# Four graph layers on one core: layer 2's squares ahead of the roots from the seventh group of a block, and four degree sums moved from layer 0 to layer 1

## The chip, the cores and the metric

The kernel runs on one core of a Trainium2 chip. The metric is the device time of one launch in microseconds (us). The kernel before took 1160.33 us (median of 3 runs, 1156.4 to 1161.47).

## The reference

Four graph layers over N = 4096 nodes with 64 features share one dense adjacency matrix `adj` (4096 x 4096, float32). Each layer takes `h = relu(layernorm(x))` and adds its result to `x`. Cut to what matters:

```
# layer 0
x = x + relu((adj @ h) @ W.T + b)
# layer 1: h, q, k are Lorentz-linear maps (each of 64 features)
att = adj * sigmoid((2 + 2 * (qm @ k.T)) / att_scale + att_bias)
support = att @ h;  x = x + support / sqrt(max(|-inner(support)|, 1e-8))
# layer 2: Poincare ball; log_ij is the log map of node j at node i
deg = max(adj.sum(axis=1), 1e-8);  w = adj / deg
agg = einsum('ij,ijc->ic', w, log_ij)     # norm of (-x_i) (+) x_j, arctanh of it, direction
x = x + expmap(0, agg @ weight + bias)
# layer 3: rank of each nonzero within its row; the last 100 weigh 0.5 ** (k - pos)
x = x + (w(rank) @ (h @ weight) + bias)
```

Layer 2 needs for every pair of nodes a scalar: with a squared distance quantity in PSUM it is worked out as square, clamp, log, square root, inverse square root (exponentials of plus and minus half the log), sum with the signed distance, log again, product. Layer 2 also needs `deg`, the row sums of `adj`. These are gathered while layers 0 and 1 read the matrix anyway.

## The kernel before, in words

The 4096 target nodes are cut into NB = 8 blocks of W = 512. The source nodes are cut into NG = 16 groups of 256 (G = 2 times 128). One adjacency tile is 128 x 2 x 512 floats, 512 KB, and belongs to one block `ib` and one group `g`.

**Tiles and loads.** `feed` (line 804) issues one DMA per tile on SyncE's queue (SP). In layers 0 and 1 the tiles live in two pools: `adjp` (6 buffers, line 156) and `adj01` (4, line 848). In each pool buffers are used in turn, and `feed` takes the pool whose oldest tile comes free first (`oldest`, line 798). A tile counts its users in `left` (`group`, line 856): its products or sums, and one more if its degree sum is made in that layer. Nineteen small DMAs for constants go out on ScalarE's queue (`constants`, line 928) while the first block runs.

**Layer 0.** `l0_sums` multiplies each tile with `h` on TensorE (PE) into an accumulator. `degree_sums(0, ...)` (line 890) adds the tile to a running tile `dg` on VectorE (DVE): a copy for a block's first tile, an addition for each further one. At a block's end `after0` (line 566) turns the sum over partitions into `deg` with one-column matmuls, and `before1` prepares layer 1's rows of this block.

**Layer 1.** `l1_atts` (PE), `l1_sigmoids` (ScalarE, ACT), `l1_weights` (DVE, `sig` times adj), `l1_sums` (PE). Some degree sums are done here: groups 3, 7, 11 and 15 (`LEFT`) of blocks 1 to 6. Where a block has such sums, `after1` (line 591) adds two `dg` halves, makes eight more one-column matmuls (each of four is issued as a pair) and adds to `deg`. The last 12 groups of layer 0 alternate with the first 12 groups of layer 1 (`EARLY`), whose blocks 0 and 1 run side by side.

**Layer 2.** The pairs are symmetric, so a block `ib` works on groups of target blocks J = ib to 7 only: 16, 14, 12, ... 2 groups, 72 in all. The first two of each block lie on the diagonal; the second of these is half as wide. Each other group is used twice: as it is, and transposed. The stages of a group:

- PE: `l2_dists` into one of two PSUM buffers `mm`; `l2_signs` into the same buffer after the square
- ACT: `l2_squares` (`v<-mm`); POOL: `l2_clamps` (`v<-v`); ACT: `l2_first_logs` (`v<-v,minus`), `l2_roots` (`t<-v`), `l2_inverses` (`v<-v`)
- DVE: `l2_coshs` (`t<-mm,t`), which frees the `mm` buffer; ACT: `l2_logs` (`t<-t`); DVE: `l2_pairs` (`t<-t,v`), `l2_weights` (`w<-t,adj`)
- PE: `l2_sums`; `l2_turns` (transposes); DVE: `l2_weights2` (`w<-tr,adj`, twice); PE: `l2_sums2`; DVE or ACT: `l2_gathers` (`others`) once per two groups

**What sets the order.** Each engine runs its instructions in program order. `in_turn` (line 733) writes this order: every stage is a thread, a cost model (`Pace`, line 60) says when each could start, and the earliest goes next. `in_steps` (line 1266) ties several threads of one engine into a fixed order per step: step k of ACT is first log k, root k, square k + 1, inverse k, log k; of DVE pair k - 1, weight k - 1, cosh k, turned weights k - 1; of PE distances k + 1, signs k, turned sums k - 2, transposes k - 1, sums k - 1. The work after a block (`after2`, `before3`) is placed between these by the planner.

Nearly all instructions are recorded by the profile under line 132, a helper that all engines share, so they are told apart by tile names.

Of the kernel before, what the change touches and what calls it, by code (L numbers as in the profile page):

```python
# [23 lines left out]
NB = N // W  # L24
CB = W // P
G = 2
NG = NC // G
LEFT = (3, 7, 11, 15)
WAIT = 0.6
EARLY = 12  # L30
BEHIND = NG - CB // G
LATE = BEHIND - CB // G
# [107 lines left out]
def kernel(ctx: ExitStack, tc: tile.TileContext, a: dict, out: bass.AP):  # L140
# [589 lines left out]
    def latest(*times):  # L730
        return None if None in times else max(times)
# [36 lines left out]
    def keep_warm(wait):  # L768


        if wait < WAIT or not spare or l1[0].get("dist") and "tables" not in opened or "third" in opened:
            return
# [69 lines left out]
    def pair_buffer(name, k):  # L842
        return pairp.tile([P, G, W], F32, tag=f"pair{k % 2}", name=name)
# [10 lines left out]


    def group(layer, ib, g):
        degree = (g in LEFT and 0 < ib < NB - 1) == (layer == 1)
        return {"layer": layer, "ib": ib, "g": g, "degree": degree, "left": 1 + degree, "at": 0.0}

    l0 = [group(0, ib, g) for ib in range(NB) for g in range(NG)]
    l1 = [group(1, ib, g) for ib in range(2) for g in range(BEHIND)]
    l1 += [group(1, ib, g) for ib in range(2) for g in range(BEHIND, NG)]
    l1 += [group(1, ib, g) for ib in range(2, NB) for g in range(NG)]
    order = l0[: len(l0) - EARLY] + [d for pair in zip(l0[len(l0) - EARLY :], l1) for d in pair]
    order += l1[EARLY:]
    done = {}
# [107 lines left out]
    def l1_sums():  # L976
        for pair in pairs:
# [24 lines left out]
    work = [  # L1002
        {"ib": i, "J": j, "half": s, "g": j * (CB // G) + s, "first": i == j and s == 0,
         "last": j == NB - 1 and s == CB // G - 1, "two": i < j, "cut": i == j and s == 1,
         "left": 1 + (i == j and s == 1), "at": 0.0}
        for i in range(NB) for j in range(i, NB) for s in range(CB // G)
    ]
# [5 lines left out]
    def part(d, t):  # L1013
        return t[:, :, OWN:] if d["cut"] else t
# [4 lines left out]
    def ago(items, k, n, what):  # L1019

        return items[k - n].get(what) if k >= n else 0.0
# [44 lines left out]
    def l2_squares():  # L1066
        for k, d in enumerate(work):
            yield "ACT", lambda: latest(
                d.get("dist"), l1[2 * k - SIG].get("summed") if 2 * k < SIG else 0.0,
                ago(work, k, SIG // 2, "paired"),  # L1070
            )
            d["v"] = pair_buffer("v", 0)
            ACT.activation(part(d, d["v"]), part(d, d["ps"]), AF.Square)
            d["square"] = pace.latest
# [19 lines left out]
    def l2_first_logs():  # L1094
        for d in work:
            yield "ACT", lambda: latest(d.get("clamped"), opened.get("tables"))
            v = part(d, d["v"])
            ACT.activation(v, v, AF.Ln, bias=minus)
            d["first_log"] = pace.latest

    def l2_roots():
        for k, d in enumerate(work):
            yield "ACT", lambda: latest(
                d.get("first_log"),
                l1[2 * k + 1 - SIG].get("summed") if 2 * k < SIG else 0.0,
                ago(work, k, SIG // 2, "weighed"), ago(work, k, SIG // 2, "turned"),
            )
            d["t"] = pair_buffer("t", 1)
            ACT.activation(part(d, d["t"]), part(d, d["v"]), AF.Exp, scale=0.5)
            d["root"] = pace.latest  # L1110

    def l2_inverses():
        for d in work:
            yield "ACT", lambda: d.get("root")
            v = part(d, d["v"])
            ACT.activation(v, v, AF.Exp, scale=-0.5)
            d["inverse"] = pace.latest
# [8 lines left out]
    def l2_logs():  # L1126
        for d in work:
            yield "ACT", lambda: d.get("read")
            ACT.activation(part(d, d["t"]), part(d, d["t"]), AF.Ln, scale=2.0 / SC)
            d["log"] = pace.latest  # L1130
# [135 lines left out]
    def in_steps(*stages):  # L1266


        parts = [next(stage[0], None) for stage in stages]
        for step in range(-1, len(work) + 3):  # L1270
            for n, (gen, behind, many) in enumerate(stages):
                k = step - behind
                for _ in range(many(work[k]) if 0 <= k < len(work) else 0):
                    yield parts[n]
                    parts[n] = next(gen, None)

    def once(d):
        return 1

# [75 lines left out]
    def l3_counts():  # L1355


        totals = []
        for h in range(2 * NB):
            half = l3[h * HG : (h + 1) * HG]  # L1360
            yield "PE", lambda: latest(*(d.get("masked") for d in half)) if spare else None
            ps = bank()
            for k in range(KH):
                for r in range(4):
                    c = 4 * k + r
                    PE.matmul(
                        ps[r * Q : (r + 1) * Q, :], pick[:, k, :],
                        half[::-1][c // G]["m"][:, c % G, :],
                        start=(k == 0), stop=(k == KH - 1), skip_group_check=True,
                    )  # L1370
            yield "DVE", lambda: ready(ps)
            totals = (totals if h % 2 else []) + [(1 - h % 2, l3_copy(f"total{h % 2}", ps))]
            yield "PE", lambda: ready(totals[-1][1]) if spare else None
            ps = bank()
            for n, (i, t) in enumerate(totals):
                PE.matmul(
                    ps, spread[:, i, :, :].rearrange("p q c -> p (q c)"), t,
                    start=(n == 0), stop=(n == len(totals) - 1),
                )
            yield "DVE", lambda: latest(ready(ps), ago(l3, h * HG, HG + 1, "ranked"))  # L1380
            chunks = l3_copy("chunks", ps)
            for d in half:
                d["chunks"] = chunks
# [72 lines left out]
    def l3_sum():  # L1456
# [22 lines left out]
        if d["last"]:  # L1479
# [6 lines left out]
        l0_sums(), l1_sums(), l1_weights(), l1_sigmoids(), l1_atts(),  # L1486
        in_steps(
            (l2_dists(), -1, once), (l2_signs(), 0, once), (l2_sums2(), 2, if_two(1)),
            (l2_turns(), 1, lambda d: 2 if d["two"] else 1), (l2_sums(), 1, once),
        ),  # L1490
        in_steps(
            (l2_first_logs(), 0, once), (l2_roots(), 0, once), (l2_squares(), -1, once), (l2_inverses(), 0, once), (l2_logs(), 0, once),
        ),
        l3_counts(),
        in_steps(
            (l2_pairs(), 1, once), (l2_weights(), 1, once),
# [50 lines left out]
```

## Time and profile before

| | us |
|---|---|
| median of 3 runs | 1160.33 |
| the profiled execution | 1154.0 |
| its span, first to last instruction | 1152.3 |
| PE matmul busy | 1076.0 (93%) |
| VectorE busy | 914.3 (79%) |
| ScalarE busy | 785.0 (68%) |
| POOL busy | 285.7 (25%) |
| DMA moved | 271.77 MB, mean 236 GB/s |
| granted TensorE clock | 0.992 |

The engines' shares are means over four layers with different limits: layer 0 to about 200 us, layer 1 to about 465, layer 2 to about 940, layer 3 to the end. So they are read by stretch. `PEld` is the weight load of TensorE, which overlaps matmuls. In lists of instructions each line gives start, duration, engine, operation, output and inputs, and in brackets the idle time before it and what ended it. "issue" in a chain is time in which the engine at that point waited for nothing that the profile shows: it was working through earlier instructions.

### The profile page before, as it was taken

The numbers are of one execution on the slowest core, as the hardware profiler recorded it, in microseconds if no ns is written. First come the engines' busy times: TensorE is split into PE (matmuls) and PEld (weight loads), VectorE is DVE, ScalarE is ACT, GpSimd is POOL, SyncE is SP. The second block draws the span as 40 slices with busy tenths as digits, with TensorE's granted clock in tenths as the row PEclk, the third lists the DMA queues.
The fourth block names the chain that finished last, engine by engine and source line by source line (L and its number), as shares of the span: only waits on it lengthen the run. The fifth ranks groups of instructions, "written<-read, shape, count | busy, mean of one in ns | idle before, by whom it ended". The sixth has DMA issues, their size and how long they took to land.

```text
span 1152.3 us, 15824 instructions
## 1 busy us (share of the span) xinstructions
PE 1076.0 (93%) x5496; PEld 451.4 (39%) x5496; DVE 914.3 (79%) x1473; ACT 785.0 (68%) x1286; POOL 285.7 (25%) x150
## 2 busy tenths in 40 slices
PE   6889999999999999999989989999999889999998
PEld 3234443333333333445434444444444433333332
DVE  7789898778888887697789888898999995555550
ACT  1145546676777667888888888897888664555554
POOL 3022222112100000254445444454445300000000
PEclk9899999999999999999999999999999999999999
DMA  7999999766677677534534535535355489888830
GB/s 277 388 384 395 409 387 357 293 217 204 213 261 241 222 236 249 175 122 161 183 132 168 197 110 186 179 128 187 124 201 173 153 351 369 321 317 321 319 114 10
DMA packets 77192, 271.77 MB, mean 236 GB/s; under 512 B 10040, under 2 KB 11064, under 8 KB 77112
## 3 DMA queue, kind: packets, MB, share of 16 engines
q1 hardware_dynamic: 75456, 270.57, 65.2%
q8 instruction: 43, 0.70, 0.2%
q10 hardware_dynamic: 1656, 0.20, 0.1%
q14 instruction: 37, 0.30, 0.1%
HBM read 269.68 MB, written 1.05 MB: 235 GB/s over the span
## 4 chain that ended last, share of the span: by engine, by line
PE 36%; DVE 18%; issue 17%; ACT 12%; POOL 11%; DMA 5%; ACTq 0%; POOLq 0%; DVEq 0%; SPq 0%
PE acc L132 15%; PE mm L132 13%; POOL v L132 10%; PE tr L132 8%; DMA adj<-in_adjT_dram 4%; ACT wt L132 3%; DVE w L132 2%; DVE sig L132 2%; DVE dg L132 2%; DVE t L132 2%; ACT v L132 2%; ACT sig L132 2%; ACT t L132 1%; DVE r_n L132 1%; POOL ln_r L132 1%
## 5 line engine op out<-in xcount | busy, mean ns | idle before, releaser
L132 PE MATMUL acc<-w,HA 128*65 128x256 f32 (+1 forms) x736 | 245.1, 468 | 15.9 <-DVE w L132 14.2
L132 POOL TENSOR_SCALAR v<-v 128x1024 f32<-128x1024 f32 x72 | 192.7, 2676 | 243.0 <-ACT v L132 238.8
L132 ACT ACTIVATE sig<-mm,att_b,att_a 128x1024 f32<-128x1024 f32 x128 | 148.9, 1200 | 53.7 <-PE mm L132 50.5
L132 ACT ACTIVATE wt<-mm 128x1024 uint16<-128x1024 f32 x124 | 120.2, 1020 | 85.4 <-PE mm L132 85.4
L132 DVE TENSOR_TENSOR sig<-sig,adj 128x1024 f32<-128x1024 f32 x128 | 152.6, 1220 | 28.5 <-ACT sig L132 26.6
L132 DVE TENSOR_TENSOR dg<-dg,adj 128x1024 f32<-128x1024 f32 x114 | 139.2, 1221 | 1.9 <-DMA adj<-in_adjT_dram 0.2
L132 PE MATMUL mm<-qT,kT 64*128 64x512 f32 x512 | 130.5, 623 | 5.9 <-ACT sig L132 5.5
L132 PEld LDWEIGHTS acc<-w,HA 128*65 128x65 f32 x736 | 93.4, 137 | 101.7 <-issue 48.1
L132 PE MATMUL acc<-adj,HA 128*64 128x512 f32 x512 | 123.3, 611 | 9.8 <-DMA adj<-in_adjT_dram 9.7
L132 PE MATMUL acc<-sig,HL 128*64 128x512 f32 x512 | 124.3, 608 | 1.5 <-DVE sig L132 1.4
L132 DVE SCALAR_TENSOR_TENSOR t<-mm,t 128x1024 f32<-128x1024 f32 x72 | 83.6, 1162 | 33.4 <-ACT t L132 24.7
L132 ACT ACTIVATE v<-v,minus 128x1024 f32<-128x1024 f32 x72 | 79.2, 1100 | 44.9 <-POOL v L132 44.4
L132 PE MATMUL acc<-wt,S 128*64 128x512 bf16 x496 | 99.2, 388 | 0.2 <-ACT wt L132 0.2
L132 DVE SCALAR_TENSOR_TENSOR t<-t,v 128x1024 f32<-128x1024 f32 x72 | 83.4, 1159 | 9.6 <-ACT t L132 9.6
L132 DVE TENSOR_TENSOR w<-t,adj 128x1024 f32<-128x1024 f32 x72 | 83.7, 1163 | 1.8
L132 DVE TENSOR_SCALAR RT<-adj 128x1024 bf16<-128x1024 f32 x74 | 51.2, 704 | 40.2 <-PE mm L132 39.1
L132 ACT ACTIVATE t<-t 128x1024 f32<-128x1024 f32 x72 | 72.1, 1001 | 12.4 <-DVE t L132 12.3
L132 PE MATMUL mm<-RT,LT 64*128 64x512 f32 (+1 forms) x288 | 78.5, 622 | 0.0
L132 DVE TENSOR_TENSOR w<-tr,adj 128x512 f32<-128x512 f32 x120 | 77.2, 680 | 0.0
L132 POOL TENSOR_TENSOR ln_r<-ln_v,minus_half 128x4 f32<-128x4 f32 x24 | 41.6, 1731 | 135.0 <-DVE ln_v L132 135.0
L132 ACT ACTIVATE t<-v 128x1024 f32<-128x1024 f32 x72 | 72.8, 1011 | 2.1
L132 PEld LDWEIGHTS mm<-qT,kT 64*128 64x128 f32 x512 | 43.3, 186 | 78.8 <-ACT sig L132 36.1
(214 smaller groups left out, 1407.6 us busy)
## 6 DMA issues: line engine op xcount, KB each, us to landing
adj<-in_adjT_dram SPq DMA_DIRECT2D x512, 512.0 KB, 4.6
x<-in_x_dram SPq DMA_DIRECT2D x4, 256.0 KB, 4.3
out_dram<-h SPq DMA_DIRECT2D x8, 128.0 KB, 2.0
b<-in_b_dram ACTq DMA_DIRECT2D x2, 32.0 KB
W<-in_W_dram ACTq DMA_DIRECT2D x3, 16.0 KB, 5.3
W0T<-in_W0T_dram ACTq DMA_DIRECT2D x2, 16.0 KB, 3.9
W1T<-in_W1T_dram ACTq DMA_DIRECT2D x1, 16.0 KB
W1T<-in_b_dram ACTq DMA_DIRECT2D x1, 0.2 KB
```

The lines of the kernel that those rows point to most:

```text
L132: done = self.tc.keep_in_program_order(getattr(self.engine, op)(*args, **kw))
```

## The change

Two things change. In `group`, block 0's degree sums of groups 4 to 7 (`FRONT`) are made in layer 1 and no longer in layer 0. In layer 2 the fixed order of ScalarE's threads is no longer written by `in_steps` but by a new thread `l2_scalars`: in the first six steps of a block (`FIRST_ROOTS`) the order is as before (first log, root, square, inverse, log), from the seventh on the square of the next group stands in front of the root (first log, square, root, inverse, log).

```
+FRONT = (4,5,6,7,)
+FIRST_ROOTS = 6
...
     def group(layer, ib, g):
-        degree = (g in LEFT and 0 < ib < NB - 1) == (layer == 1)
+        degree = (g in (LEFT if ib else FRONT) and ib < NB - 1) == (layer == 1)
...
+    def l2_scalars():
+        logs1, squares, roots = l2_first_logs(), l2_squares(), l2_roots()
+        inverses, logs2 = l2_inverses(), l2_logs()
+        parts = {t: next(t) for t in (logs1, squares, roots, inverses, logs2)}
+        k = 0
+        for step in range(-1, len(work)):
+            d = work[max(step, 0)]
+            k = 0 if d["first"] else k + 1
+            order = [logs1, squares, roots, inverses, logs2]
+            if 0 <= k < FIRST_ROOTS:
+                order[1:3] = roots, squares
+            for t in order if step >= 0 else [squares]:
+                if parts[t] is not None:
+                    yield parts[t]
+                    parts[t] = next(t, None)
...
-        in_steps(
-            (l2_first_logs(), 0, once), (l2_roots(), 0, once), (l2_squares(), -1, once), (l2_inverses(), 0, once), (l2_logs(), 0, once),
-        ),
+        l2_scalars(),
```

## The prediction

> **What bounds the kernel now.** I read the chain that ended last, then the same chain in a window of layer 2, then each engine's own list of instructions there, and last the busy times by stretch. The chain of the whole page is mixed:
>
> ```profile
> PE 36%; DVE 18%; issue 17%; ACT 12%; POOL 11%; DMA 5%; ACTq 0%; POOLq 0%; DVEq 0%; SPq 0%
> ```
>
> In layer 2 it is not mixed. Between 612 and 650 us the chain is one pattern, repeated (start, duration, what):
>
> ```profile
> 618.86 2.77 POOL v L132
> 621.62 3.23 issue
> ...
> 624.89 2.76 POOL v L132
> 627.65 3.22 issue
> ```
>
> The period is 624.89 - 618.86 = 6.03 us. The "issue" of 3.23 us is work on ScalarE (start, duration, operation):
>
> ```profile
> 642.99 2.77 POOL L132 TENSOR_SCALAR v<-v 128x1024 f32<-128x1024 f32 x1 [3.27 <-ACT v L132]
> ...
> 645.79 1.15 ACT L132 ACTIVATE v<-v,minus 128x1024 f32<-128x1024 f32 x1 [0.99 <-POOL v L132]
> 646.97 1.06 ACT L132 ACTIVATE t<-v 128x1024 f32<-128x1024 f32 x1
> 647.93 1.01 ACT L132 ACTIVATE v<-mm 128x1024 f32<-128x1024 f32 x1
> 648.84 1.05 ACT L132 ACTIVATE v<-v 128x1024 f32<-128x1024 f32 x1
> 649.78 1.05 ACT L132 ACTIVATE t<-t 128x1024 f32<-128x1024 f32 x1
> ```
>
> So: clamp of group k on POOL, first log (1.18 to the next start), root (0.96), square of group k+1 (1.01), 0.08 to the next clamp. The loop is clamp, log, root, square, clamp; ScalarE then idles 0.99 us for POOL. TensorE is close behind:
>
> ```profile
> 643.53 1.13 PE L132 MATMUL mm<-RT,LT 64*128 64x512 f32 x4
> ...
> 649.38 1.13 PE L132 MATMUL mm<-RT,LT 64*128 64x512 f32 x4
> ```
>
> This period has no recorded idle time and is 5.85 us; the one before it took 6.19.
>
> Layer 0's start is bound by transfers:
>
> ```profile
> 20.13 4.73 DMA adj<-in_adjT_dram
> 24.94 6.32 DMA adj<-in_adjT_dram
> 32.80 8.30 DMA adj<-in_adjT_dram
> ```
>
> By stretch (us; PE, PEld, DVE, ACT, POOL busy; clock; DMA share; GB/s):
>
> ```profile
> 18.00:35.00 17.00, 9.16 (x30) 1.64 (x28) 16.59 (x15) 0.20 (x1) 1.36 (x1) 0.82 0.66 222
> 60.00:178.00 118.00, 114.03 (x618) 52.19 (x620) 106.79 (x187) 58.41 (x229) 28.38 (x29) 1.00 1.00 392
> 178.00:200.00 22.00, 21.38 (x106) 8.01 (x102) 20.26 (x26) 15.56 (x55) 5.93 (x3) 1.00 0.94 365
> 613.00:661.00 48.00, 47.43 (x227) 22.93 (x225) 40.78 (x45) 39.82 (x41) 21.94 (x8) 1.00 0.52 181
> ```
>
> At 18-35 us DMA moves 222 GB/s and VectorE is full of degree sums; to 178 us DMA is saturated, and around 190 us PE and VectorE are both full.
>
> **Layer 2: the square before the root.** The new order holds in the step of each group from a block's seventh on: 10, 8, 6, 4 and 2 steps of blocks 0 to 4 (16, 14, 12, 10, 8 groups), 30 of 72. Block 0's first two take 7.41 and 7.83 us now, filled by the tail of layer 1; I give these nothing. 28 periods of 6.03 are left. Nothing is added or removed; three things move.
>
> - The POOL loop loses the root: 2.80 (clamp to log) + 1.18 + 1.01 + 0.08 = 5.07 us.
> - ScalarE: counted from the first log, the square starts at 1.18, the root at 2.13 (ends 3.19, 0.95 later than now), the inverse root at 3.08. The second log would start at 4.03, but needs VectorE's `t<-mm,t` (`l2_coshs`): 3.22 to 4.44. So the change adds a wait of about 0.45 us before the second log, at 4.48. Behind it on ScalarE stand the next first log and square, and POOL's next clamp. The next first log starts at 5.43 (its clamp has ended at about 5.1), so ScalarE allows 5.45.
> - VectorE: 1.25 + 1.25 + 1.14 + 1.27 = 4.9 us, 0.6 more in every second group (`others`), avg 5.2.
> - PE, from start to start in the 5.85 period: sums 1.72, distances and signs 1.38, turned sums 1.78, transposes 0.88: 5.76. The missing 0.09 is the wait of the distances for `t` of two groups before.
>
> The longest is PE's 5.76. 28 x (6.03 - 5.76) = 7.6 us. There is an effect at the edges. The root comes 0.95 us later, so in a block's first changed step PE's distances (3.80 after the first log now) come at 4.74: PE loses 0.95. ScalarE meanwhile runs ahead at 5.45 until the square must wait for the distances, some 0.7 us of lead. At the block's end PE trails by that sum; in the list at 661-670 us PE idles 0.72 and 1.31 us for VectorE and VectorE paces the step, so the lag fits in and ScalarE's lead is kept: 0.27n + 0.70 for n = 8, 8, 6, 4, and 1.2 for n = 2, together 11.0 us. With 5.85, the shortest whole period that the trace shows, it is about 8. I take **9.5 us**. If PE's lag is not absorbed, each block pays 0.95: 7.6 - 4.8 = 2.8.
>
> Two rules of the Trainium skill would change this. "SBUF — State Buffer" (Who interferes with whom) says that a VectorE instruction with two SBUF inputs and a GpSimd instruction that reads SBUF exclude each other for the whole instruction. A clamp pushed back by one such operation (1.22) makes the loop 5.07 + 1.22 = 6.29, and the change loses 0.26 x 28 = 7 us. Against it stands the row: the clamp at 642.99 runs to 645.76 while `t<-t,v`, both inputs in SBUF, starts at 644.83 and takes its usual 1.23; both have their usual length. I follow the row. "Perfetto Trace Analysis" (Identifying the Most-Contended Engine) says that matmul busy share misjudges TensorE and weight loads are the better measure: 22.93 of 48 us here. By that PE has room, ScalarE's 5.45 would decide, and the gain would be 28 x 0.58 = 16 us. But the starts themselves lie back to back over 5.85 us, so I stay with PE.
>
> **The degree sums of block 0, groups 4 to 7.** Layer 0 loses four additions of 1.22 (4.9 us of VectorE). Their tiles come free once PE has summed them, by 18.2 us, instead of after VectorE, which starts the sums at 17.79. DMAs are the same in number and size; what moves is their place in SP's queue. Landings are 1.28 us apart when DMA is full, but from the tenth tile (19.1) to the sixteenth (34.6) they took 15.5 instead of 7.7: 7.8 us lost. Groups 4 and 5 stand behind 0 to 3 in their pool of six; 6 and 7 are the oldest of the pool of four, so two loads can go out at once: 2 x 1.28 = 2.6 us. The loads after them still pass between the constants' small DMAs (19 on ScalarE's queue), so I don't take all. Ends: 0 and 7.8. DMA is the limit to 178 us, so what is won lasts till there.
>
> Layer 1 takes one copy (0.69) and three additions: 4.35 us of VectorE, plus 0.68 and 0.16 in `after1`, eight one-column matmuls on PE and a small copy on ScalarE. PE's part has no cover (213 of 220 us busy from 240 to 460): `after1` with them takes 1.87, without 1.10, so 0.77. VectorE's part has cover only in gaps: it has none from 177 to 198.5 us, then 2.2, 0.5 and 2.0 before 214. Behind it wait the `sig` products and the degree sums of layer 0's last block. The tiles are held longer, four of ten. Ends: 0 if all fall in gaps, 4.35 + one stalled tile of 4 us. I take 1.3; with PE 2.1. Net of the move: **+0.5 us**.
>
> **The sum.** 9.5 + 0.5 = 10 us off the profiled execution of 1154.0 (span 1152.3): 1144. That execution is 6.3 below the median of 1160.33; the difference carries over: 1160.3 - 9.8, **1150.5 us**.
>
> **Rivals.**
> 1. *PE paces, the lag stays.* Layer 2 gives 2.8, the move nothing: 1157.5. For it: PE is 99% busy from 613 to 661; against it: its idle spots right after each block. Chance 0.17.
> 2. *The move costs layers 0 and 1.* VectorE has no gap at 177-198 us, four tiles are kept: 7 us lost, 9.5 won below: 1158. Against it: DMA at 74% from 200 on. Chance 0.10.
> 3. *Slower: the later root becomes the chain.* Second log, pair, weight, cosh, second log is 1.05 + 1.25 + 1.25 + 1.22 = 4.8 us, with the turned weights between up to 5.5. The bound decides if something pushes it over 6.03, say a gather and a layer-normalisation piece placed before the cosh. At 6.3 it costs 28 x 0.27 + 5 x 0.95 = 12: 1172. Against it: 0.5 us of slack. Chance 0.13.
>
> **Chances and range.** My forecast has 0.60, with its own range 1146 to 1155. An effect under 0.5% (5.8 us) can't be told from none here. Faster: 0.60, nearly all of the forecast (a few hundredths at its slow end traded against the fast ends of rivals 1 and 2). Within: 0.24. Slower: 0.16, rival 3 and the tail of rival 2. The range 1145 to 1166 takes in the forecast and rivals 1 and 2 and leaves out rival 3.
>
> **What would show it.** Right: from 613 to 661 us the clamps lie 5.75 to 5.85 apart, the clamp starts one log and one square after the last ends, the second log waits about 0.4 us for `t`, and PE's idle time in changed steps is gone; tiles 10 and 11 land before 22.5 us. Wrong: a period still at 6.0 with the wait now before PE's distances; longer intervals in groups 0 to 5; `sig` products late near 200 us with PE waiting for adj.

## The result and the profile after

The kernel after takes 1155.99 us (median of 20 runs, 1149.82 to 1164.91). The kernel before takes 1160.9 us (20 runs, 1155.64 to 1169.78). The ratio on record is 0.9948, with a 95% interval of 0.9927 to 0.9969, so 6.0 us less (3.6 to 8.5); the two medians differ by 4.9. The forecast was 1150.5, so 9.8 less, in a range of 1145 to 1166: the sign and the range hold, the size came out at about six tenths by the ratio and at half by the medians.

The profiled execution of the kernel after took 1157.54 us (span 1155.8), which is longer than the one before (1154.0, span 1152.3). Its mean granted clock was 0.985 instead of 0.992, and over all timed runs of this study the time falls by about 0.85 us for each thousandth of mean clock (one common slope fitted to the runs of all kernels). Seven thousandths are 6 us, so the two spans can't be compared as they stand. Within a stage at full clock they can.

The mix of the chain that ended last has changed. POOL had 11% of it and has 7; PE had 36 and has 41:

```profile
PE 41%; DVE 19%; ACT 14%; issue 13%; POOL 7%; DMA 6%; ACTq 0%; POOLq 0%; SPq 0%; DVEq 0%
```

**Block 0 of layer 2 does what the prediction said.** In POOL's own list (start, duration, and in brackets the idle time before it) the clamps lie 5.85 us apart, not 6.03:

```profile
555.92 2.77 POOL L134 TENSOR_SCALAR v<-v 128x1024 f32<-128x1024 f32 x1 [3.08 <-ACT v L134]
561.78 2.77 POOL L134 TENSOR_SCALAR v<-v 128x1024 f32<-128x1024 f32 x1 [3.09 <-ACT v L134]
```

ScalarE's list there no longer shows an idle time before the first log (`v<-v,minus`), where it waited 0.99 us for POOL. It now waits 0.45 us before the square, for PE's distances:

```profile
546.44 1.04 ACT L134 ACTIVATE t<-t 128x1024 f32<-128x1024 f32 x1
547.38 1.14 ACT L134 ACTIVATE v<-v,minus 128x1024 f32<-128x1024 f32 x1
548.97 1.02 ACT L134 ACTIVATE v<-mm 128x1024 f32<-128x1024 f32 x1 [0.45 <-PE mm L134]
```

PE's list shows the reason. From one group's distances (`mm<-RT,LT`) to the next it has no idle time in 547.48 - 541.63 = 5.85 us:

```profile
541.63 1.13 PE L134 MATMUL mm<-RT,LT 64*128 64x512 f32 x4
542.69 0.39 PE L134 MATMUL mm<-RB,LB 32*128 32x512 bf16 x4
543.02 1.94 PE L134 MATMUL acc<-w,HA 128*65 128x256 f32 x8
544.80 1.04 PE L134 MATMUL tr<-ident,t 128*128 128x128 f32 x8
545.67 1.88 PE L134 MATMUL acc<-w,HA 128*65 128x512 f32 x4
547.48 1.13 PE L134 MATMUL mm<-RT,LT 64*128 64x512 f32 x4
```

**Blocks 1 to 4 do not.** In block 1 the first three changed intervals are short (4.95, 5.24 and 5.38 us), while ScalarE takes its lead over PE. Then the clamps lie 6.87, 5.85, 6.39 and 5.85 us apart, where before each period was 6.03. They no longer take 2.77 us each, either:

```profile
631.84 3.46 POOL L134 TENSOR_SCALAR v<-v 128x1024 f32<-128x1024 f32 x1 [2.27 <-ACT v L134]
638.71 2.77 POOL L134 TENSOR_SCALAR v<-v 128x1024 f32<-128x1024 f32 x1 [3.42 <-ACT v L134]
644.56 2.97 POOL L134 TENSOR_SCALAR v<-v 128x1024 f32<-128x1024 f32 x1 [3.08 <-ACT v L134]
650.95 2.77 POOL L134 TENSOR_SCALAR v<-v 128x1024 f32<-128x1024 f32 x1 [3.42 <-ACT v L134]
```

The waits of that stretch (620 to 663 us; who waited for whom: total, times, longest) name something that was not there before. PE waits for the addition into `others`, and ScalarE for PE:

```profile
ACT v L134 <- PE mm L134: 4.2, 5, 1.1
...
PE acc L134 <- DVE others L134: 2.0, 3, 1.0
```

In the order of all engines' instructions one sees why. VectorE adds to `others` between the pair (`t<-t,v`) and the weight (`w<-t,adj`), and PE's turned sums, which need the accumulator that this addition reads, start only when it is done:

```profile
654.20 1.23 DVE L134 SCALAR_TENSOR_TENSOR t<-t,v 128x1024 f32<-128x1024 f32 x1
655.34 0.68 DVE L134 TENSOR_TENSOR others<-acc,others 65x512 f32<-65x512 f32 x1
655.69 1.02 ACT L134 ACTIVATE v<-mm 128x1024 f32<-128x1024 f32 x1 [0.48 <-PE mm L134]
655.94 1.21 DVE L134 TENSOR_TENSOR w<-t,adj 128x1024 f32<-128x1024 f32 x1
656.17 1.91 PE L134 MATMUL acc<-w,HA 128*65 128x256 f32 x8 [0.51 <-DVE others L134]
```

In the kernel before, the same addition stood right behind the cosh (`t<-mm,t`), ahead of the turned weights and of the pair, some 2.4 us earlier in VectorE's step:

```profile
648.06 1.22 DVE L132 SCALAR_TENSOR_TENSOR t<-mm,t 128x1024 f32<-128x1024 f32 x1 [0.74 <-ACT t L132]
649.20 0.68 DVE L132 TENSOR_TENSOR others<-acc,others 65x512 f32<-65x512 f32 x1
649.80 1.27 DVE L132 TENSOR_TENSOR w<-tr,adj 128x512 f32<-128x512 f32 x2
```

No line of the change moves it. `l2_gathers` is a thread outside the fixed steps, so `in_turn` places it where its cost model finds it first possible, and with ScalarE's new order that was another place. In block 0 the gather is a copy on ScalarE, so the block escapes.

**The start of layer 0.** From 18 to 35 us (busy us and number of instructions of PE, weight load, VectorE, ScalarE, POOL; clock; DMA share; GB/s) VectorE is busy 3 us less than the 16.59 before, and the loads are no faster (222 GB/s before):

```profile
18.00:35.00 17.00, 8.71 (x32) 1.73 (x30) 13.42 (x13) 0.20 (x1) 1.28 (x1) 0.84 0.69 220
```

VectorE now waits for loads instead of loads for VectorE:

```profile
DVE dg L134 <- DMA adj<-in_adjT_dram: 3.2, 1, 3.2
```

Added up from the packets of the tiles' queue (512 KB each), the eleventh, twelfth and thirteenth tile land at about 20.4, 22.5 and 24.9 us instead of 21.9, 24.6 and 27.8. Then the loads fall behind again: the seventeenth lands at 36.6 us, before at 36.0.

### The profile page after: what moved, and what is told of

It reads as the page before. It is cut to its first block, busy times and chain, and to the rows that moved or that the text cites. A ratio compares the mean times of both kernels' runs of the same rounds, so it can differ in the third digit from the quotient of the medians.

```text
span 1155.8 us, 15839 instructions
## 1 busy us (share of the span) xinstructions
PE 1084.9 (94%) x5510; PEld 456.7 (40%) x5510; DVE 911.2 (79%) x1475; ACT 788.2 (68%) x1287; POOL 285.2 (25%) x150
## 4 chain that ended last, share of the span: by engine, by line
PE 41%; DVE 19%; ACT 14%; issue 13%; POOL 7%; DMA 6%; ACTq 0%; POOLq 0%; SPq 0%; DVEq 0%
PE acc L134 18%; PE mm L134 15%; PE tr L134 8%; POOL v L134 5%; DMA adj<-in_adjT_dram 5%; DVE w L134 4%; ACT v L134 4%; ACT t L134 3%; ACT wt L134 3%; DVE dg L134 3%; DVE t L134 3%; DVE sig L134 2%; ACT sig L134 1%; ACT lo_sq L134 1%; DVE others L134 1%
## 5 line engine op out<-in xcount | busy, mean ns | idle before, releaser
L134 POOL TENSOR_SCALAR v<-v 128x1024 f32<-128x1024 f32 x72 | 195.8, 2719 | 242.7 <-ACT v L134 229.3
L134 ACT ACTIVATE v<-mm 128x1024 f32<-128x1024 f32 x72 | 69.7, 968 | 18.5 <-PE mm L134 18.5
```

Source lines behind the costliest of these rows:

```text
L134: done = self.tc.keep_in_program_order(getattr(self.engine, op)(*args, **kw))
```

## The experiments

Two theories stood after this reading. **A**: PE's 5.85 us is the floor of the new order, and the displaced addition takes back nearly all of the gain in blocks 1 to 4. **B**: the later root itself makes a slower chain there (rival 3 of the prediction), or the degree sums cost what layer 2 wins (rivals 1 and 2). Each group below says what its runs decide. "At equal clock" means the difference that is left after taking 0.85 us per thousandth of mean clock out of every run; its standard error is 0.4 to 0.7 us, and it is the better number where clocks differ by chance. If a change itself moves the clock, it leaves that part out.

**The two parts apart.** First the new order alone, with the degree sums where they were:

```
-        degree = (g in (LEFT if ib else FRONT) and ib < NB - 1) == (layer == 1)
+        degree = (g in LEFT and 0 < ib < NB - 1) == (layer == 1)
```

> Only layer 2's new order; all degree sums of block 0 stay in layer 0. Theory A (the gain is made in layer 2, in block 0): 2.3 to 4 us under the kernel before, the same as the whole change within 2 us; clamps of block 0 at 5.85 us, of block 1 alternating 5.85 and 6.40. Theory B (half of the change's gain is the moved degree sums): at most 1.5 us under the kernel before.

Measured: 1157.08 us, ratio 0.9958 (0.9936 to 0.998); at equal clock -2.6 us, against -3.4 for the whole change. Then the reverse, on the kernel before: `FRONT` and the line of `group` above with it, nothing else.

> Only the four degree sums moved; layer 2 in the old order. Theory A: within 1.5 us of the kernel before; the seventeenth tile lands at 36 to 37 us as before, since the constants' DMAs hold up the loads and not VectorE. Theory B: 2.5 us or more under it. The prediction's own term was 0.5 us faster.

Measured: 1162.68 us, ratio 1.0005 (0.9985 to 1.0025); at equal clock +0.3. So the move of the degree sums is worth nothing that these runs can tell from zero, either way, and the gain is the order's.

**The addition put back behind the cosh.** In blocks 1 and later the gather becomes part of VectorE's fixed step; block 0's copy on ScalarE stays with the planner:

```
-    def l2_gathers():
+    def l2_gathers(on_v):
         for d in twos:
-            if d["half"] == 0:
+            if d["half"] == 0 or (d["ib"] > 0) != on_v:
                 continue
...
             (l2_coshs(), 0, once),
+            (l2_gathers(True), 2, lambda d: 1 if d["two"] and d["half"] and d["ib"] else 0),
             (l2_weights2(), 1, ...
...
-        l2_clamps(), l2_gathers(), l3_weights(), ...
+        l2_clamps(), l2_gathers(False), l3_weights(), ...
```

> The changed kernel, with VectorE's addition into others (blocks 1 to 6) fixed behind the cosh of the step, ahead of the turned weights, instead of wherever the planner puts it. Theory A (the addition between pair and weight lets TensorE wait 0.5 us in every second group): clamps of block 1 at 5.85 throughout, each of blocks 1 to 3 some 1 to 2 us shorter, 3 to 5 us under the changed kernel. Rival (TensorE is full and the lag at a block's end costs what the steps win): periods of 5.85 too, but the gain is lost again in the first four groups of the next block, under 1 us.

Measured: 1148.34 us, ratio 0.9880 (0.9845 to 0.9916); at equal clock -10.1. The addition stands behind the cosh again, and no matmul waits for it:

```profile
648.03 1.23 DVE L134 SCALAR_TENSOR_TENSOR t<-mm,t 128x1024 f32<-128x1024 f32 x1 [1.01 <-ACT t L134]
649.17 0.68 DVE L134 TENSOR_TENSOR others<-acc,others 65x512 f32<-65x512 f32 x1
649.77 1.27 DVE L134 TENSOR_TENSOR w<-tr,adj 128x512 f32<-128x512 f32 x2
```

Behind the same three short intervals the clamps of block 1 are now 5.85 apart throughout:

```profile
635.44 2.77 POOL L134 TENSOR_SCALAR v<-v 128x1024 f32<-128x1024 f32 x1 [2.29 <-ACT v L134]
641.29 3.07 POOL L134 TENSOR_SCALAR v<-v 128x1024 f32<-128x1024 f32 x1 [3.09 <-ACT v L134]
647.14 2.77 POOL L134 TENSOR_SCALAR v<-v 128x1024 f32<-128x1024 f32 x1 [2.77 <-ACT v L134]
652.99 3.08 POOL L134 TENSOR_SCALAR v<-v 128x1024 f32<-128x1024 f32 x1 [3.08 <-ACT v L134]
```

Is that the undisturbed new order, or would the same edit help by itself? The gather edit on the kernel before, with the old order:

> The kernel before with only the addition into others fixed behind the cosh. If the addition's place matters only under the new order (the old one is bound by the loop over POOL), clamps stay 6.03 us apart and the time is within 1.5 us of the kernel before. If the fixed place is worth something by itself, periods fall below 6.0 and it is 3 us or more faster.

Measured: 1163.6 us, ratio 1.0012 (0.9993 to 1.003); at equal clock +0.3. And the edit with the new order but without the moved degree sums (the line of `group` as in the first run):

> The kernel with the fixed addition, with all of block 0's degree sums back in layer 0. If the moved sums are worth nothing, as when moved alone, the time is that of the kernel with the fixed addition within 2 us, so 12 to 15 us under the kernel before. If the move is worth something once layer 2 is fast, it is 3 us or more above it.

Measured: 1149.11 us, ratio 0.9862 (0.9821 to 0.9904); at equal clock -9.9. So the gain needs the new order and the fixed addition together, and does not need the move. The time from a block's first clamp to the next block's (in the last row to the last clamp of all), from the starts in POOL's list (us), shows where it lies:

| block (changed steps) | before | after | addition fixed | half of turned sums | new order from the fifth group |
|---|---|---|---|---|---|
| 0 (10) | 99.02 | 97.10 | 96.68 | 94.33 | 98.54 |
| 1 (8) | 84.31 | 83.88 | 81.77 | 81.59 | 82.37 |
| 2 (6) | 72.68 | 72.54 | 70.72 | 71.03 | 71.24 |
| 3 (4) | 60.62 | 60.31 | 59.02 | 59.94 | 59.55 |
| 4 (2) | 48.54 | 48.68 | 47.80 | 48.82 | 47.89 |
| 5 (0) | 37.51 | 38.89 | 38.64 | 38.58 | 37.81 |
| 6 and 7 (0) | 30.97 | 30.98 | 30.98 | 31.79 | 34.04 |
| sum | 433.65 | 432.38 | 425.61 | 426.08 | 431.44 |

(Of block 0's time after, 1.0 us is a stretch at a lower clock near its start: the interval behind its second clamp took 5.50 instead of 4.49 us, at a clock of 0.51 instead of 0.71. The last two columns are runs that follow.)

**Is PE the floor?** With the addition fixed, matmuls fill 44.86 of 44.90 us, and weight loads 21.36:

```profile
614.00:658.90 44.90, 44.86 (x213) 21.36 (x212) 39.78 (x44) 39.95 (x40) 23.95 (x9) 1.00 0.50 180
```

A full list alone proves little, since the ends of matmuls are modelled in these profiles. A run on that kernel takes half of each turned sum away, so the changed steps carry 0.86 us less of PE's work and the same work on all other engines:

```
-            for k in range(CB):
+            for k in range(CB // 2):
...
-                    start=(k == 0), stop=(k == CB - 1),
+                    start=(k == 0), stop=(k == CB // 2 - 1),
```

> As the kernel with the fixed addition, but only two of the four source chunks of each turned sum are multiplied (the turned half of layer 2's result is incomplete), which takes 0.86 us from TensorE in every step. If TensorE sets the 5.85 us of the changed steps, the period falls to 5.4 to 5.5, where ScalarE and the waits for the cosh should set it by the prediction's count. If something else sets it, it stays at 5.85.

One run: 1147.93 us. In block 0 the clamps move from 5.85 to 5.27 apart:

```profile
553.10 3.06 POOL L134 TENSOR_SCALAR v<-v 128x1024 f32<-128x1024 f32 x1 [2.18 <-ACT v L134]
558.36 3.11 POOL L134 TENSOR_SCALAR v<-v 128x1024 f32<-128x1024 f32 x1 [2.20 <-ACT v L134]
```

So PE did set the 5.85. The next bound is 0.6 us behind it: by stretch, ScalarE is now busy 15.77 of 16.00 us (fourth pair of numbers):

```profile
552.00:568.00 16.00, 15.82 (x75) 6.85 (x74) 14.58 (x16) 15.77 (x19) 9.23 (x3) 1.00 0.61 230
```

PE still reads 15.82, though each step has 0.86 us less for it: a list of PE without gaps does not say by itself that PE sets the pace.

From block 1 on, where the addition is VectorE's, the steps alternate between 5.86 and 5.23 and the clamps between 3.68 and 2.77 us. For every second clamp the trace names VectorE's weight as what ended its wait, not the square:

```profile
638.84 3.68 POOL L134 TENSOR_SCALAR v<-v 128x1024 f32<-128x1024 f32 x1 [2.47 <-ACT v L134]
644.71 2.76 POOL L134 TENSOR_SCALAR v<-v 128x1024 f32<-128x1024 f32 x1 [2.18 <-DVE w L134]
```

The table shows that taking this PE work away is worth 2.35 us in block 0, while the rest takes 2.8 us longer. A single run can't carry a difference of a microsecond; the intervals in the trace can.

**How early can the new order begin?** With the addition fixed, the new order from the third group of a block on (`FIRST_ROOTS = 2`):

> As the kernel with the fixed addition, but the square goes in front from a block's third group on. If groups 2 to 5 are bound by VectorE and the tail of the block before (intervals of 6.5, 7.1 and 6.0), the new order only adds the later root there: no more than 1 us of gain, or a loss of up to 3 us. If they too are bound by the loop over POOL, each block gains another 0.5 to 1 us, 3 to 6 us in all.

Measured: 1168.26 us, ratio 1.0076 (1.0039 to 1.0112); at equal clock +8.4. In blocks 1 to 5 the interval behind the fourth group is 9.67 us, where the other runs have 7.1 (the half-turned one 6.9 in block 1). ScalarE's list there (block 1) shows the second log (`t<-t`) behind the end of the previous block's `after2` (until 601.83), and the square not much later than it was:

```profile
601.74 1.04 ACT L134 ACTIVATE t<-t 128x1024 f32<-128x1024 f32 x1
602.68 1.13 ACT L134 ACTIVATE v<-v,minus 128x1024 f32<-128x1024 f32 x1
...
604.22 1.01 ACT L134 ACTIVATE v<-mm 128x1024 f32<-128x1024 f32 x1
```

The square has ended at 605.23, but its clamp starts at 607.53, because POOL has a piece of the layer norm in front of it, and this waits for VectorE:

```profile
605.67 1.87 POOL L134 TENSOR_TENSOR ln_r<-ln_v,minus_half 128x4 f32<-128x4 f32 x1 [5.05 <-DVE ln_v L134]
607.53 2.77 POOL L134 TENSOR_SCALAR v<-v 128x1024 f32<-128x1024 f32 x1
```

That is 2.3 of the 2.57 us. From the seventh group on, this piece stands behind the clamp (601.95 to 604.68, `ln_r` at 604.68, with the addition fixed). So in blocks 1 to 5 the loss is again an instruction that the planner placed elsewhere, not ScalarE's chain. Blocks 6 and 7 lose another 5.0 us (36.0 instead of 31.0), which was not traced. From the fifth group on (`FIRST_ROOTS = 4`):

> The kernel with the fixed addition, and the new order from a block's fifth group on. When it began with the third, only the interval after the fourth group grew (9.7 instead of 7.1) while the next two shrank from 6.0 to 5.1 and 5.2. If the harm is in that one step, clamps of the fifth and sixth groups come 5.0 to 5.3 apart and 1 to 4 us are gained. If TensorE's lag takes it back, within 1 us of the fixed addition; if the tail of the block before is pushed into the steps again, 5 us or more slower.

Measured: 1155.38 us, ratio 0.9948 (0.9925 to 0.9971); at equal clock -4.3, so some 6 us worse than from the seventh on. The last column of the table has it: two more changed steps save nothing in blocks 0 to 4 (in blocks 1 to 4 the lead they give, 4.94 in place of 6.04, is spent again in the next step, 6.3 to 6.4), and blocks 6 and 7 pay 3.1 us. With four and two groups these have no changed step of their own; why they pay stays open.

**What holds the loads at the start.** If VectorE's degree sums hold tiles and so loads, fifteen of block 0's sixteen sums moved to layer 1 should free them (`FRONT = tuple(range(15))`, on the kernel before):

> The old order, and fifteen of block 0's sixteen degree sums moved to layer 1, so that VectorE holds back no tile of the first block. If VectorE's sums held up the loads, tiles 10 to 16 land about 1.3 us apart and the seventeenth tile by 30 us. If the constants' small DMAs do, the seventeenth still lands at 35 to 38 us. Layer 1 is expected to be 5 to 15 us longer for the fifteen additions; the total is not the point.

One run: 1172.45 us. VectorE is nearly idle in the window (third pair), and the rate rises from 222 to 242 GB/s only:

```profile
18.00:35.00 17.00, 9.97 (x36) 1.83 (x32) 1.39 (x2) 0.20 (x1) 1.39 (x1) 0.85 0.69 242
```

SyncE's queue then spends most of the stretch waiting for earlier loads to land (total, times, longest):

```profile
SPq L813 <- DMA adj<-in_adjT_dram: 15.4, 5, 4.5
```

The seventeenth tile lands at 34.4 us, 1.6 earlier, and the whole run is longer. The other suspects were the nineteen small DMAs of the constants, and two of their properties were to be tried on the kernel before. First their turn among the completion semaphores, which they share with the tiles, by planning them all at once:

```
-            yield "ACT", lambda: 20.0 + 0.5 * k
+            yield "ACT", lambda: 15.0 + 0.05 * k
```

> The kernel before, with the constants' 19 small DMAs planned in one clump, so that each queue keeps its order and only the turn in which DMAs of the two queues share completion semaphores changes. If the shared semaphores hold up the tile loads of the first block, tiles 10 to 16 land less than 2 us apart on average (2.4 before) and the time falls by 2 to 5 us. If VectorE's degree sums hold them up, nothing changes (within 1 us).

Measured: 1163.02 us, ratio 1.0002 (0.9981 to 1.0024), with 210 GB/s in the window. But this edit left what it was to change as it was. In its trace the constants go out from 15.81 to 29.5 us (before: 15.73 to 28.8), and the loads between them take the same semaphores in the same order. So the run decides nothing. And as early as they can go (`6.0 + 0.1 * k`):

> The kernel before with the constants' 19 small DMAs issued early, among the squares of the first layer normalisation, while VectorE cannot start its degree sums anyway. If these DMAs hold up tile loads wherever they run, the first ten tiles land later (by 2 to 6 us) and tiles 10 to 16 land about 1.3 us apart, or as fast as VectorE frees them. If not, tiles 10 to 16 still take 15 us.

One run: 1168.54 us. This run is inconclusive too. The constants' issues got between ScalarE's squares of the first layer norm, so VectorE came late as well, and either could explain the low rate:

```profile
18.00:35.00 17.00, 8.33 (x28) 2.30 (x28) 10.21 (x14) 1.35 (x3) 3.89 (x2) 0.70 0.38 116
```

The runs show that VectorE's sums alone do not hold these loads. The trace of the kernel before says more. From 18 to 35 us SyncE's queue waits once for VectorE, then for other tiles and for two constants, which no tile needs:

```profile
SPq L812 <- DVE dg L132: 8.8, 1, 8.8
SPq L812 <- DMA adj<-in_adjT_dram: 8.0, 5, 2.8
SPq L812 <- DMA scal<-in_att_scale_dram: 1.2, 1, 1.2
SPq L812 <- DMA W0T<-in_W0T_dram: 1.2, 1, 1.2
```

The packed trace names the semaphore that each DMA counts up when it lands: eight of them, which the DMAs of both queues take in turn. From 20 to 32 us each tile load goes out just after the previous user of its semaphore has landed: at 20.13 (a constant, landed 20.06), 22.31 (a tile, 22.16), 24.94 (a tile, 24.87), 28.22 (a tile, 28.13), 29.93 (a constant, 29.84) and 31.35 (a tile, 31.26). The constants have the other turns, so from 20 us to the load of 29.93 two tile loads are in flight at a time. As an estimate from this trace, two loads of 512 KB that take 4.74 us each (the one of 20.13) make 221 GB/s; 222 were measured. With fifteen sums moved it is the same: 22.48 behind 22.43, 23.91 behind 23.84, 26.08 behind 26.02. So the shared semaphores set when these loads go out. What it costs was not measured, since no run gives the constants semaphores of their own.

## Why the prediction was right, and where not

**The total is in part luck.** The change was to give nearly 10 us, 9.5 of them in layer 2, and gave 3.4 at equal clock. The other 2.5 of the measured 6.0 go with a higher mean clock, for which the prediction has no term. (In its sum, 9.5 + 0.5 is 10, and it takes 9.8 off: a slip that decides nothing.)

**"The POOL loop loses the root": right.** The clamp starts one log and one square after the last ends (2.2 us of idle time where nothing else is late). In block 0 the period is no longer POOL's.

**"The longest is PE's 5.76": right engine, size off.** PE back to back takes 5.85 in the kernel after and with the addition fixed. The missing 0.09 was not a wait that goes away. Over 28 periods that is 2.5 us; the prediction had this case beside its own ("with 5.85 about 8"), and the kernel with the fixed addition gives 433.65 - 425.61 = 8.04 us.

**"0.6 more in every second group (`others`), avg 5.2": the step that failed.** VectorE's time was added up and found short enough. Its place in the order was taken as fixed, but it is the planner's, and from block 1 on it came to stand where PE needs the accumulator. In block 1 PE waits 1.0 us the first time and 0.5 us in every second group after it, and there the steps take 5.85 and 6.40, on average 6.12: more than the 6.03 before. At equal clock the whole change gives 3.4 us, and with only this addition moved back 10.1. So the step cost 6.7 us, more than two thirds of the 9.5 expected of layer 2. Without the moved degree sums the same edit gives 7.3 (2.6 and 9.9).

**ScalarE's second log** waits 0.20 us for `t` (0.45 forecast), so ScalarE's bound is lower than 5.45: 5.27 in the run with half of the turned sums.

**The edges: the right number in block 0 by other terms, too kind after.** From block 0's seventh group to block 1's first the kernel after needs 60.56 us, before 63.50: 2.94 won, 2.86 forecast. The six steps at 5.85 give 1.1 of it and the four before them 1.8, where the forecast had 2.2 (eight times 0.27) and 0.7. And the next block's first steps give 0.9 back. With the addition fixed, block 1 shows both: its eight steps take 44.81 us instead of 48.25, a lead of 3.4, and the three intervals around the change of blocks take 18.42 instead of 17.31, so 1.1 is lost. The forecast let PE's lag fit wholly into idle time there. The lead was 2.0 (4.94, 5.24 and 5.38 against 5.85) and not 0.70, and the loss was not zero; that together they come to the 8 of the prediction's other case is luck.

**The degree sums, "+0.5": right by offsetting nothings.** The 2.6 us of earlier loads did not come, since the loads behind the two early ones wait for the completion semaphores again. The 2.1 us in layer 1 did not show in the total either. "Tiles 10 and 11 land before 22.5 us" says little: counted from one they did so before the change too (19.1 and 21.9), counted from zero they land at 20.4 and 22.5. The seventeenth tile was the one to name.

**The rivals.** Rival 1 has the right engine and, with 1157.5 us, a time nearer to the measured 1155.99 than the forecast's own 1150.5, but its mechanism (PE's lag kept at each block) accounts for the 0.9 to 1.1 us that each block gives back, not for what was lost inside the blocks. Rival 2 is refuted by the move alone (1.0005). Rival 3 named the very thing, "a gather ... placed before the cosh", and gave it 0.13; it weighed it for ScalarE's chain and not for PE's accumulator, so its price, 12 us, was too high for this case. No run shows that chain at 6.03 or more; ScalarE comes to set the pace only at 5.27, with half of the turned sums. The slower run, with the new order from the third group on, lost some 2.3 us in each of blocks 1 to 5 behind `ln_r` on POOL.

**The two rules.** Weight-load share as the measure of TensorE would have called for 16 us. Weight loads were busy about half of the time (21.36 of 44.90 us) while PE set the pace, and taking PE's work away shortened the period, so setting the weight loads aside was right. For the exclusion of VectorE and POOL the prediction followed one row and dropped the rule. That row was of an instruction that starts 1.84 us into the clamp. The rule does act on those that meet near a clamp's start (last section); in the steady steps of block 0 it happens to cost nothing.

**What stays open.** The ratio says 6.0 us, the layer-2 traces differ by 1.3, or 2.3 without the stretch at a lower clock. At equal clock 3.4 are left. The other 2.5 go with the mean clock, 0.9863 over the runs of the kernel after and 0.9834 over those before. Leaving out those with a single run, the kernels with the new order in this study had 0.9850 to 0.9875, those with the old one 0.9823 to 0.9841. Taken together this is 0.9859 (78 runs) against 0.9834 (173), and the standard error of the difference is 0.0006, so chance alone is unlikely. If the order raises the clock, the 2.5 us are its own; how it would do so was not tried. With the fixed addition, too, the runs show some 2 us more than the clamps.

**A version that beats both** is the new order with the addition in VectorE's fixed step, with the moved degree sums or without: 1148.34 and 1149.11 us.

## What to carry to other kernels

A change of one engine's order changes the order of every instruction that a planner places freely on the others; so list those (here the addition on VectorE and `ln_r` on POOL), ask which of them the next bound waits for, and fix their place in the step. When a loop is opened, work out the next bound in each regime (block 0 with its copy on ScalarE, later blocks with an addition on VectorE) rather than with an average. An engine that a trace shows back to back has the period that its starts show, gaps included: 5.85 was in the profile, 5.76 was a sum. That it also sets the pace takes a run with less work for it. And before a run counts as a test, look in its trace whether the edit changed what it was meant to change.

## What the runs showed of the hardware that was not expected

- **A clamp on POOL and a VectorE instruction with both operands in SBUF hold each other up, whichever comes second, but only near the clamp's start.** The clamp at 631.84 overlaps the weight `w<-t,adj` (631.46 to 632.67) by 0.83 us and takes 3.46 in place of 2.77; the one at 626.46 overlaps one by 0.49 and takes 3.11; the one at 644.56 by 0.35 and takes 2.97. The excess is the overlap less about 0.15. Overlaps of up to 1.16 us with `t<-mm,t`, which has one operand in PSUM, leave the clamp at 2.77 in 17 of 18 cases (one took 3.08). The other way round, a weight that starts just after a clamp is the one that is held (run with half of the turned sums):

```profile
666.61 2.77 POOL L134 TENSOR_SCALAR v<-v 128x1024 f32<-128x1024 f32 x1 [3.17 <-DVE r_sq L134]
666.80 1.93 DVE L134 TENSOR_TENSOR w<-t,adj 128x1024 f32<-128x1024 f32 x1
```

  It takes 1.93 in place of 1.22 us, and so do the four others of that run; one that starts 0.04 us after a clamp takes 2.07 (new order from the fifth group). All end about 2.1 us after the clamp's start, as if they had begun 0.9 us into it. Those that start 1.24 us or more into a clamp keep their length, like the one at 644.83 in the profile before. So the Trainium skill's rule in "SBUF — State Buffer" (Who interferes with whom) holds in both orders here, but a clamp holds VectorE for the first 0.9 of its 2.77 us only (the page says "for the whole instruction" of VectorE's two-port modes; the prediction took it for this pair as well). The new order, which starts clamps earlier, meets it more often: 16 of 64 clamps last over 2.8 us, before 7.
- **Time goes with the granted clock from execution to execution.** The kernel after took about 1150 us at a mean clock of 0.991 and 1165 at 0.977. The stretches at lower clock differ from trace to trace: from 480 to 500 us, at the start of layer 2, the clock is 0.91 in the profile before and 0.83 in the one after.
- **Loads on one queue can be held up by small DMAs on another through shared completion semaphores.** At 18 to 35 us the tiles move at 192 to 242 GB/s in all runs but the one with early constants, whether VectorE is full or idle, and from 60 to 178 us at 392 in the kernel before. In the kernel before, each load of 20 to 32 us starts 0.05 to 0.15 us after the DMA that had its semaphore before it has landed, be it a tile or a constant. That this wait makes the low rate is inferred from these times; no run takes it away.
